# Attention inside a four-part network: denominators from two running totals, counted every sixteen key tiles, two halves of weighted sums between the score sets

## The chip, the cores and the metric

One core of a Trainium2 chip runs the whole network as one program. The metric is the device time of one execution in microseconds. The kernel before took 9539.7 us (median of three runs, 9533.88 to 9544.37).

PE is the matrix engine, PEld its loading of weights, DVE the vector engine, ACT the scalar engine (activations such as the exponential), POOL the general engine, SP the engine that issues transfers. Matmuls write to PSUM[...]; the other engines work between PSUM and the on-chip memory.

## The reference

The input is four images of 64 x 64 pixels with 128 channels. Four stages follow one another, each adding to its input: attention, a recurrent layer, a selective scan, and a mixture of experts. Only attention concerns us here. It normalises the channels, then for four heads of 32 channels:

```
q, k, v = split(x @ w_qkv)                  # 4096 tokens per image
q, k    = l2norm over the tokens (axis 1)
sim     = einsum('bihd,bjhd->bhij', q, k) * 10
attn    = softmax(sim, axis=-1)
out     = einsum('bhij,bjhd->bhid', attn, v)
x       = x + out @ w_out + b_out
```

So for each image and head there are 4096 x 4096 exponentials, a weighted sum of `v` by them, and for each query the sum of its exponentials, the denominator.

## The kernel before, in words

All is fp32 and lies with channels, or keys, on the partitions. A first part normalises and makes q, k and v of all images. The second part, `attend`, takes each image's queries in eight chunks of 512 (`c`), and for each chunk its keys in 32 tiles of 128 (`t`). That is 4 x 8 x 32 = 1024 tiles, each with four units, one for each head. This part's instructions are placed on each engine in the order in which the code emits them (the schedule is written by hand), so the loop's order is the order of the work. The maximum is not subtracted; a bound on the scores that is worked out first lets the small-score version run.

The loop runs in turns. In a turn, `scores("sa", 4)` (L288) makes the next four units' scores, each a matmul of 32 rows, into a tile of four PSUM banks, and one ACT instruction (L303) writes their exponentials into a ring in the on-chip memory. The ring has places for 8 tiles (`RING`) of four heads, 32 places in all, and a set that crosses its end takes two ACT instructions. Then come `halves(BETWEEN)`, the weighted sums (L313): for each tile, two halves of 256 queries, four matmuls each, one for each head. The second part of the turn is `scores("sb", 3)`, a set of three units into three banks, followed by the halves that are left of the turn's four (`HEADS - n`). [...]`sa`, `sb` and `av` have one buffer each: a new set waits until ACT has read the last one. `state["halves"]` rations the halves to the scores made: a full turn makes seven units, which pay for three and a half halves, so turns with four halves alternate with shorter ones.

The denominators go another way. `added` (called for each tile whose scores are done) lets DVE add the tile's 128 x 2048 exponentials into a total: the first two tiles of each eight make it (L332), each further one is added in place (L336). After every `SUMMED` = 8 tiles the total is due to be counted, `LATER` = 3 turns on: in that turn the tile `sb` is not used for scores but for `counted` (L341), four matmuls of the total with ones, which sum over the keys on the partitions. ACT copies the sum to `den` (L351 for a chunk's first count, L353 for the next ones), and DVE adds the later ones up (L354). When a chunk's last total is counted, DVE takes the reciprocal (L358) and multiplies the weighted sum by it (L359), and the next counting turn also holds the projection by `w_out` (L365), with its bias on ACT (L368), the addition of `x` on DVE (L372) and the store (L373).

The ring ties the engines: a place is written again eight tiles later, and before that DVE must have added the tile and PE must have used it.

Of the kernel before, what the change touches and what calls it, by code (L numbers as in the profile page):

```python
# [19 lines left out]
F32 = mybir.dt.float32  # L20
# [6 lines left out]
P = 128  # L27
B, HW, C = 4, 64, 128
L = HW * HW
CH = 512  # L30
# [3 lines left out]
HEADS, DH = 4, 32  # L34
# [131 lines left out]
@with_exitstack  # L166
def attention(ctx, tc, a, x1):

    nc = tc.nc
    flag = ctx.enter_context(tc.tile_pool(name="at_f", bufs=1)).tile(
        [1, 1], mybir.dt.int32, name="flag"
    )
    with ExitStack() as inner:
        attention_of_small(inner, tc, a, x1, flag)
    with tc.If(nc.values_load(flag) > 0):  # L180
        attention_of_any(tc, a, x1)


def attention_of_small(ctx, tc, a, x1, flag):

    nc = tc.nc
    cst = ctx.enter_context(tc.tile_pool(name="at_c", bufs=1))
    NJ = L // P
    RING = 8
    LATER = 3  # L190
    SUMMED = 8
    BETWEEN = 3

    ident = cst.tile([P, P], F32, name="ident")
    make_identity(nc, ident)
# [68 lines left out]
    def attend(stream, work, ps):  # L264
# [11 lines left out]
        def scores(tag, size):  # L276

            s = ps.tile([P, size, CH], F32, tag=tag, name=tag)
            n0, m, done = state["n"], 0, []
            for _ in range(size):  # L280
                unit = next(units, None)
                if unit is None:
                    state["over"] = True
                    break
                chunk_state, t, i = unit
                q, k = chunk_state["qk"]
                rows = slice(DH * i, DH * i + DH)
                nc.tensor.matmul(  # L288
                    s[:, m, :],
                    k[rows, tokens(t)],  # L290
                    q[rows, chunk(chunk_state["c"])],
                    start=True,
                    stop=True,
                )
                m += 1
                if i == HEADS - 1:
                    done.append((chunk_state, t, place(n0 + m - HEADS)))
            state["n"] += m
            at = 0
            while at < m:  # L300
                lo = place(n0 + at)
                n = min(m - at, RING * HEADS - lo)
                nc.scalar.activation(ring[:, lo : lo + n, :], s[:, at : at + n, :], AF.Exp)  # L303
                at += n
            return done
# [18 lines left out]
        def added(chunk_state, t, at):  # L324

            w = ring[:, at : at + HEADS, :]
            g = t % SUMMED
            if g == 0:
                chunk_state["first"] = w
            elif g == 1:  # L330
                total = work.tile([P, HEADS, CH], F32, tag="total", name="total")
                nc.vector.tensor_add(total, chunk_state["first"], w)  # L332
                chunk_state["total"] = total
            else:
                total = chunk_state["total"]
                nc.vector.tensor_add(total, total, w)  # L336
            return g == SUMMED - 1

        def counted(slot, chunk_state, t, total):
            for i in range(HEADS):  # L340
                nc.tensor.matmul(  # L341
                    slot[DH * i : DH * i + DH, 0, :], ones, total[:, i, :], start=True, stop=True
                )
            return lambda: taken(slot, chunk_state, t)

        def taken(slot, chunk_state, t):
            if t < SUMMED:
                chunk_state["den"] = work.tile([P, 2, CH], F32, tag="den", name="den")
            den = chunk_state["den"]
            if t < SUMMED:  # L350
                nc.scalar.copy(den[:, 0, :], slot[:, 0, :])  # L351
            else:
                nc.scalar.copy(den[:, 1, :], slot[:, 0, :])  # L353
                later.append(lambda: nc.vector.tensor_add(den[:, 0, :], den[:, 0, :], den[:, 1, :]))  # L354
# [22 lines left out]
        def halves(limit):  # L377

            n = 0
            while n < limit and state["halves"] > 0 and ready:  # L380
                half = state["half"]
                if n and half == 0 and ready[0][1] == 0:
                    break
                tile = ready[0]
                weighted(half, *tile)
                whole = tile[1] == 0
                if half or whole:
                    ready.pop(0)
                state["half"] = 0 if whole else 1 - half
                state["halves"] -= 4 if whole else 2  # L390
                n += 2 if whole else 1
            return n
# [5 lines left out]
        while ready or to_count or to_divide or to_project or later or not state["over"]:  # L398
            turn += 1
            before = state["n"]  # L400
            done = [] if state["over"] else scores("sa", 4)
            n = halves(BETWEEN)
            ending = state["over"] and not ready and not to_count
            counting = to_count and to_count[0][0] <= turn
            if counting or (to_project and ending):
                slot = ps.tile([P, 3, CH], F32, tag="sb", name="sb")
                after = []
                if counting:
                    _, chunk_state, t, total = to_count.pop(0)
# [13 lines left out]
            for tile_done in done:  # L423
                if added(*tile_done):
                    chunk_state, t, _ = tile_done
                    to_count.append((turn + LATER, chunk_state, t, chunk_state["total"]))
            ready += done
# [1421 lines left out]
```

## Time and profile before

| what | number |
|---|---|
| median of three runs | 9539.7 us |
| the profiled execution's own time | 9539.87 us |
| its span | 9538.1 us |
| PE, DVE, ACT, POOL busy, share of the span | 92%, 88%, 72%, 54% |
| granted PE clock, mean | 0.969 |
| attention's score sets, first and last start | 233.4 and 2627.8 us |
| L336 adds, mean | 768, 2290 ns |
| L332 adds, mean | 128, 2288 ns |
| L303 exponentials of `sa`, mean | 640, 1879 ns |
| L303 exponentials of `sb`, mean | 512, 1452 ns |

Attention with its preparation is the first 2640 us or so of the span; the rest is the other three stages, which the change does not touch. The busy shares of the whole page are means over all stages, so what follows looks at attention alone. A line number is the place in the code from which an instruction comes. A group's row gives the busy time, the mean of one, and the idle time of the engine just ahead of it with what ended it. A matmul in fp32 shows as two records. "issue" is time in which an engine waited for nothing that the profile shows.

### The profile page before, as it was taken

What the parts mean: (1) busy time and instruction counts of PE and PEld (TensorE: products, weight loads), DVE (VectorE), ACT (ScalarE), POOL (GpSimd) and SP (SyncE); (2) the same over time, 40 slices, a digit from 0 to 9 for tenths busy, and PEclk for the clock granted to TensorE, in tenths of its full rate; (3) what the DMA queues carried; (4) which work ended last, traced back from release to release, by engine and by line L of the source; (5) the groups of instructions that cost most, each with busy time, mean ns of one, the idle gap of its engine ahead of it and who ended that gap; (6) DMA issues with size and microseconds to landing.
All of it is one profiled execution on the core that took longest, in us unless ns stands there. A gap on an engine that the chain in (4) does not pass through costs nothing. (4 is left out here: it accounts for less than half of the span.)

```text
span 9538.1 us, 238512 instructions
## 1 busy us (share of the span) xinstructions
PE 8769.6 (92%) x102706; PEld 4347.9 (46%) x102706; DVE 8353.8 (88%) x5099; ACT 6913.6 (72%) x10362; POOL 5157.2 (54%) x2433
## 2 busy tenths in 40 slices
PE   7999999999988888999999999999999999999766
PEld 3333333333323334555555555555555555555223
DVE  6999999999978218999999999999999999999764
ACT  3888888888856457777778877877777777777321
POOL 0000000000001017999999999999999999999100
PEclk8999999999999888999999999999999999999887
DMA  4001000000011335666666666666666666665634
GB/s 173 29 8 37 8 8 34 8 10 8 8 60 51 114 135 150 169 170 170 170 168 161 161 159 159 160 168 171 170 171 170 170 171 171 170 170 164 228 118 182
DMA packets 530961, 1164.79 MB, mean 122 GB/s; under 512 B 76818, under 2 KB 444506, under 8 KB 502106
## 3 DMA queue, kind: packets, MB, share of 16 engines
q1 hardware_dynamic: 529882, 1149.30, 41.6%
q8 instruction: 811, 13.29, 0.6%
q14 instruction: 268, 2.20, 0.1%
HBM read 828.51 MB, written 182.15 MB: 106 GB/s over the span
## 5 line engine op out<-in xcount | busy, mean ns | idle before, releaser
L1288 DVE TENSOR_TENSOR_SCAN states<-decays,db 128x1016 f32<-128x1016 f32 x2112 | 4668.6, 2256 | 100.3 <-ACT decays L1309 60.9
L1322 POOL TENSOR_TENSOR products<-states,c_ring 128x1000 f32<-128x1000 f32 x2112 | 4456.9, 2151 | 219.2 <-PE y L1339 190.4
L1229 ACT ACTIVATE decays<-dt,a_logs 128x500 f32<-128x500 f32 x4224 | 3017.2, 714 | 90.3 <-DVE states L1288 4.2
L1264 PEld LDWEIGHTS db<-b_diag,dtu_t 32*128 32x128 f32 x16896 | 2050.0, 186 | 1607.6 <-DVE states L1288 1187.7
L1264 PE MATMUL db<-b_diag,dtu_t 32*128 32x128 f32 x16896 | 2428.6, 283 | 316.2 <-DVE states L1288 310.5
L1264 PE MATMUL db<-b_other,dtu_t 32*128 32x128 f32 x16896 | 2457.4, 284 | 0.0
L1273 PE MATMUL y<-zeros 32*128 32x128 f32 x14720 | 2122.3, 283 | 0.0
L1264 PEld LDWEIGHTS db<-b_other,dtu_t 32*128 32x128 f32 x16896 | 2048.8, 186 | 0.1
L1339 PE MATMUL y<-products,ident 64*64 64x500 f32 x16896 | 2019.1, 592 | 1.1 <-POOL products L1322 1.1
L336 DVE TENSOR_TENSOR total<-total,ring 128x2048 f32<-128x2048 f32 x768 | 1759.1, 2290 | 66.8 <-DVE total L336 2.3
L1273 PEld LDWEIGHTS y<-zeros 32*128 32x128 f32 x14720 | 1772.1, 186 | 0.0
masks.py:197 POOL MEMSET ident<- 128x128 f32 x6 | 1.2, 205 | 2940.3 <-SPq L180 2647.1
L303 ACT ACTIVATE ring<-sa 128x2048 f32<-128x2048 f32 x640 | 1202.8, 1879 | 159.5 <-PE sa L288 159.4
L313 PE MATMUL av<-ring,v_at 128*32 128x256 f32 (+1 forms) x16128 | 1094.3, 388 | 0.4 <-ACT ring L303 0.4
L313 PEld LDWEIGHTS av<-ring,v_at 128*32 128x32 f32 x16128 | 432.1, 109 | 941.4 <-issue 745.6
L1339 PEld LDWEIGHTS y<-products,ident 64*64 64x64 f32 x16896 | 541.3, 132 | 696.8 <-issue 568.2
L303 ACT ACTIVATE ring<-sb 128x1536 f32<-128x1536 f32 x512 | 743.6, 1452 | 124.7 <-PE sb L288 109.7
L1309 ACT COPY decays<-states 128x8 f32<-128x8 f32 x2048 | 405.2, 198 | 535.1 <-DVE states L1288 519.0
L288 PE MATMUL sa<-q_at,k_at 32*128 32x512 f32 x5120 | 732.2, 641 | 17.0 <-issue 14.1
L288 PE MATMUL sb<-q_at,k_at 32*128 32x512 f32 x3072 | 582.1, 641 | 0.0
L332 DVE TENSOR_TENSOR total<-ring 128x2048 f32<-128x2048 f32 x128 | 292.9, 2288 | 114.6 <-ACT ring L303 114.6
L288 PEld LDWEIGHTS sa<-q_at,k_at 32*128 32x128 f32 x5120 | 201.0, 183 | 378.5 <-ACT ring L303 205.6
(210 smaller groups left out, 7952.9 us busy)
## 6 DMA issues: line engine op xcount, KB each, us to landing
c_ring<-c_rows SPq DMA_DIRECT2D x2112, 250.0 KB, 4.6
b_other<-b_diag SPq DMA_DIRECT2D x264, 512.0 KB, 6.4
weights<-in_w SPq DMA_DIRECT2D x32, 1024.0 KB, 12.6
u<-u_r SPq DMA_DIRECT2D x60, 500.0 KB, 5.6
y_r<-sum SPq DMA_DIRECT2D x60, 500.0 KB, 4.2
u<-u_c SPq DMA_DIRECT2D x60, 500.0 KB, 5.6
y_c<-sum SPq DMA_DIRECT2D x60, 500.0 KB, 4.1
x<-x SPq DMA_DIRECT2D x96, 256.0 KB, 2.6
```

What stands on the lines that cost most here:

```text
L288: nc.tensor.matmul(s[:, m, :], k[rows, tokens(t)], q[rows, chunk(chunk_state["c"])], start=True, stop=True,)
L303: nc.scalar.activation(ring[:, lo : lo + n, :], s[:, at : at + n, :], AF.Exp)
L313: nc.tensor.matmul(chunk_state["av"][rows, some], chunk_state["v"][:, t, rows], ring[:, at + i, some], start=t == 0, stop=t == NJ - 1 and ...
L332: nc.vector.tensor_add(total, chunk_state["first"], w)
L336: nc.vector.tensor_add(total, total, w)
L1229: nc.scalar.activation(to, dt, AF.Exp, scale=scale)
L1264: nc.tensor.matmul(bank.rearrange("p (n t) -> p n t", n=4)[:, :, to : to + 32], v.dtu[rows, h, s, :], b[rows, s, 4 * self.q : 4 * self.q + ...
L1273: nc.tensor.matmul(y[:, idle // 2, :P], zeros[rows], zeros[rows], start=False, stop=False)
L1288: nc.vector.tensor_tensor_scan(order(self.slot(states)), order(self.slot(decays, shift)), order(self.db[:, SKIP + shift :][:, : 2 * LANE]) ...
L1309: nc.scalar.copy(self.edge(later.slot(decays), later.v.into), last)
L1322: nc.gpsimd.tensor_mul(to, h, c)
L1339: nc.tensor.matmul(to, ident[rows, rows], of, start=begins, stop=ends)
```

## The change

Three constants change. `SUMMED` goes from 8 to 16 tiles, so that a chunk has two counts instead of four. `LATER` goes from 3 to 4 turns. `BETWEEN`, the most halves of weighted sums between the two score sets of a turn, goes from 3 to 2; the other two may follow behind the second set.

Within each sixteen tiles there are two totals, one for even and one for odd tiles. Tiles 0 and 1 are only remembered; tile 2 makes the even total from tiles 0 and 2, tile 3 the odd one from 1 and 3; later tiles are added to the two in turn; behind tile 15 one more add joins the two. The even total has two buffers and the odd one a single buffer, each of 128 x 2048; `den` goes from two buffers to one.

```
-    LATER = 3
-    SUMMED = 8
-    BETWEEN = 3
+    LATER = 4
+    SUMMED = 16
+    BETWEEN = 2
...
             g = t % SUMMED
             if g == 0:
-                chunk_state["first"] = w
-            elif g == 1:
-                total = work.tile([P, HEADS, CH], F32, tag="total", name="total")
-                nc.vector.tensor_add(total, chunk_state["first"], w)
-                chunk_state["total"] = total
-            else:
-                total = chunk_state["total"]
-                nc.vector.tensor_add(total, total, w)
-            return g == SUMMED - 1
+                chunk_state["sums"] = []
+            sums = chunk_state["sums"]
+            if g < 2:
+                sums.append(w)
+                return False
+            if g < 4:
+                total = work.tile(
+                    [P, HEADS, CH], F32, tag=f"total{g}", name=f"total{g}", bufs=4 - g
+                )
+                nc.vector.tensor_add(total, sums[g - 2], w)
+                sums[g - 2] = total
+                return False
+            nc.vector.tensor_add(sums[g % 2], sums[g % 2], w)
+            if g < SUMMED - 1:
+                return False
+            nc.vector.tensor_add(sums[0], sums[0], sums[1])
+            chunk_state["total"] = sums[0]
+            return True
...
             if t < SUMMED:
-                chunk_state["den"] = work.tile([P, 2, CH], F32, tag="den", name="den")
+                chunk_state["den"] = work.tile([P, 2, CH], F32, tag="den", name="den", bufs=1)
```

## The prediction

> **What bounds the kernel now.** The change touches only the attention stage, so I asked first where that stage lies and which engine is full in it. The busy time by stretches (length, then busy time and instruction count of each engine) puts it between about 219 us and 2640 us of the 9538.1 us span:
>
> ```profile
> core 0: us, PE busy (x) PEld busy (x) DVE busy (x) ACT busy (x) POOL busy (x), PEclk, DMA share, GB/s
> ...
> 600.00:1000.00 400.00, 400.00 (x4252) 138.82 (x4247) 373.14 (x183) 338.05 (x226) 0.00 (x0) 1.00 0.07 24
> 1000.00:1400.00 400.00, 399.73 (x4244) 138.67 (x4240) 374.54 (x183) 337.89 (x225) 0.00 (x0) 1.00 0.03 9
> ```
>
> PE never rests, DVE is at 93%, ACT at 84%, PE's clock is granted in full and DMA does nearly nothing. Next, the groups by line within 300 to 2600 us (xcount | busy us, mean ns of one | idle before):
>
> ```profile
> L336 DVE TENSOR_TENSOR total<-total,ring 128x2048 f32<-128x2048 f32 x738 | 1690.3, 2290 | 63.2 <-DVE total L336 2.3 <-ACT den L351 0.5 <-DVE total L332 0.5
> L303 ACT ACTIVATE ring<-sa 128x2048 f32<-128x2048 f32 x615 | 1155.8, 1879 | 153.6 <-PE sa L288 153.6
> ...
> L303 ACT ACTIVATE ring<-sb 128x1536 f32<-128x1536 f32 x492 | 714.6, 1452 | 117.7 <-PE sb L288 103.1
> L288 PE MATMUL sa<-q_at,k_at 32*128 32x512 f32 x4920 | 701.3, 640 | 1.1 <-ACT ring L303 1.1
> ...
> L332 DVE TENSOR_TENSOR total<-ring 128x2048 f32<-128x2048 f32 x123 | 281.4, 2288 | 86.9 <-ACT ring L303 86.9
> ```
>
> PE waited 1.1 us in 2300 for score banks; ACT and DVE wait for PE and for ACT. So PE's order of work sets the stage's length. Since matmul ends are modelled, I take PE prices from the starts in the timeline (start, duration, engine, line, group, count):
>
> ```profile
> 1006.50 1.14 PE L288 MATMUL sa<-q_at,k_at 32*128 32x512 f32 x8 [0.27 <-ACT ring L303]
> ...
> 1007.57 1.50 PE L313 MATMUL av<-ring,v_at 128*32 128x256 f32 x24
> ...
> 1008.21 2.28 DVE L336 TENSOR_TENSOR total<-total,ring 128x2048 f32<-128x2048 f32 x1
> 1009.00 1.13 PE L288 MATMUL sb<-q_at,k_at 32*128 32x512 f32 x6
> ...
> 1010.06 0.64 PE L313 MATMUL av<-ring,v_at 128*32 128x256 f32 x8
> ...
> 1010.41 2.28 DVE L332 TENSOR_TENSOR total<-ring 128x2048 f32<-128x2048 f32 x1
> 1010.63 1.14 PE L288 MATMUL sa<-q_at,k_at 32*128 32x512 f32 x8
> ...
> 1012.80 7.09 DVE L336 TENSOR_TENSOR total<-total,ring 128x2048 f32<-128x2048 f32 x3
> ...
> 1013.02 1.04 PE L341 MATMUL sb<-total,ones 128*32 128x512 f32 x8
> ...
> 1013.99 0.30 PEld L365 LDWEIGHTS sb<-o,wo 128*128 128x128 f32 x2 [0.84 <-issue]
> ```
>
> From start to start: a set of scores 1.07 us, whether of four or of three; three halves of weighted sums 1.43, one half 0.57, so 0.43 a half and 0.14 for each group of halves. A turn of set, three halves, set, one half is 4.13; over the stage such turns have a median of 4.14, turns of set, two halves, set 3.15, turns with a count instead of the second set (three halves before it, one after) 3.79, with count and projection 4.99. A count thus costs 3.79 - (1.07 + 1.43 + 0.57) = 0.72, a projection 1.20.
>
> On DVE the same rows show the point about running totals: from an add to a later instruction that does not read its result (L336 at 1008.21 to L332 at 1010.41) 2.20 us; from L332 to the L336 that reads its result 2.39. Over the stage 127 L332-to-L336 steps have a median of 2.39, and an L336 behind a small instruction, which waits for a total finished long before, starts 0.60 us after a 0.68 us add: a wait that is already met costs nothing.
>
> **What the Trainium skill says.** "VectorE: DVE Perf Modes", The TRN2 errata: an fp32 tensor add takes (N+151)/0.96 ns, 2291 at N=2048; the trace has 2290. Its table's 58+N cycles, 2194 ns, fits the trace's 2.20 of an independent follower. The same page, The DRAIN you can't avoid, says a semaphore between two operations costs nothing extra; the trace says 0.19 us (2.39 against 2.20) where it is the result just written, and the trace decides. "ScalarE: Activation LUTs", What ACT_TABLE_LOAD costs: an activation takes 186 ns + 0.833 ns an element, consecutive ones overlapping by some 93 ns; the trace has 1879 (1892 by the formula), and its two sizes give 1452 - 3 x 427 = 171 ns fixed.
>
> **The change, part by part.** The numbers of instructions are from the order of the instructions in the two programs.
>
> 1. Counts on PE: 128 become 64, and each count's turn loses a three-score set. Turns go from 640 to 613, sets from 640+512 = 1152 to 613+549 = 1162. Score matmuls (4096) and halves (2048) are unchanged; groups of halves go from 1022 to 1023. So -64 x 0.72 = -46.1 us and +10 x 1.07 = +10.7 us. The 64 ACT copies (0.59 us) and 64 DVE adds of `den` (0.60 us) that go with them are off PE's path.
>
> 2. BETWEEN 3 to 2: the turn patterns become 365 of 2+2 halves, 181 of 2+0, 45 count turns with 2+2, 18 with 2+0, in place of 256 of 3+1, 255 of 2+0 and 127 count turns of 3+1. A 2+2 turn is 1.07+1.00+1.07+1.00 = 4.13 (rounding), the same as 3+1; the halves only move. The second set directly ahead of the first costs some 0.02 more (3.17 mean against 3.15), 74 times fewer: -1.5 us.
>
> 3. Where PE meets ACT anew: `sa` and `sb` have one buffer each. In a 2+0 turn the next `sa` comes 3.15 us after the last one; that one's exponentials start some 1.21 us after their set and take 1.88, so it is just met, as today. Three new cases are not met. A 2+0 turn behind a 2+0 turn (9 times): exponentials start 0.27 later, stall some 0.25. A count turn with no halves behind it (18 times): next set due at 2.82 to 2.93 against 3.15, stall some 0.3. And the ring's places no longer repeat with the pattern: 90 of the 1162 sets now straddle the ring's end and take two activations, adding 171 ns less the overlap of some 0.1; about a tenth of the 181 tight turns are hit. Together 2 + 5 + 3 = +10 us. The extra ACT work itself (90 x 0.08 = 7 us) hides in ACT's 16% idle.
>
> 4. Adds on DVE: 7 per eight tiles become 15 per sixteen, 896 to 960. Before: 128 x (6 x 2.39 + 2.20) = 2117 us; small instructions 96 x 0.60 + 32 x (3.38 + 0.61 + 0.60) = 204; each of those 160 breaks a chain and saves 0.19, -30: 2291. After: even and odd totals alternate, so 64 x (14 x 2.20 + 2.39) = 2124, small instructions 32 x 0.60 + 147 = 166: 2290. The extra adds are paid by the removed waits. This is the least certain price, since no run shows two alternating totals: bounds 2.20 and 2.39, taken 2.20.
>
> 5. What DVE's lateness can hold up. Setting the adds against the exponentials tile by tile, DVE ends a tile's add 2.3 to 8.2 us after its exponentials (8.2 behind a division), and the ring place is rewritten at least 8.1 us after that. Holding tiles 0 and 1 until tiles 2 and 3 costs one more tile, 2.3 us: still free. LATER 4: the last add plus the merging add of 2.2 to 2.4 ends at most some 10 us behind the exponentials; the count comes four turns on, about 15 us: no wait. `den` with one buffer: the copy for the next chunk comes over ten tiles behind the division: no wait. At the very end the merging add is exposed, about +1 us.
>
> Sum: -46.1 + 10.7 - 1.5 + 10 + 1 = -26 us; 2 us more where a count runs straight into a score set. Against the profiled 9539.87 us, which equals the median of 9539.7 within 0.2, that is some 9512. Work outside the stage is unchanged.
>
> **Rivals.**
> - A, likeliest, 0.77: as summed, 9500 to 9521, the ends being no new ACT stalls (-38) and twice as many (-17).
> - B, no change, 0.13: PE's saving is given back because score sets and exponentials mesh worse: if all 90 straddling sets stall PE 0.15 (+13) and the tight turns that follow another short turn lose 0.5, the gain is some 12 us: 9528. For it: ACT and PE run within 0.1 us of each other in 2+0 turns. Against it: there are fewer such turns than before.
> - C, slower, 0.08: DVE becomes the bound. If each alternating add still costs 2.39, DVE needs 64 x 15 x 2.39 + 166 = 2460 us, and the stage ends near 242 + 2460 = 2702 instead of 2645: 9597. It decides from 2.31 us per add: the adds now run from 242 to 2635, and 64 x (14p + 2.39) + 166 fills those 2393 us at p = 2.31. Against it are the steps of 2.20 and of 0.60 above.
> - D, larger gain, 0.02: 9495, if counts free ACT and DVE in ways that the turn prices miss.
>
> **How the numbers follow.** A difference under 0.2%, 19 us, can't be told from none. A's bulk lies under 9520.6; a small part of it counts as no change. Faster: 0.75 of A and D; same: 0.16; slower: 0.09. The likeliest is 9512; the range 9499 to 9530 holds A and B's centre, and leaves out C and D.
>
> **What would show it.** The profile after should have 64 counts, 613 and 549 score sets, PE still at 99% in the stage, which ends some 26 us sooner; adds on DVE 2.20 us apart with 2.39 only at the merging add; some 90 split activations; waits of `sa` for the ring's exponentials not above some 15 us in PE's own idle. Adds 2.39 apart and PE idle ahead of the counts (L350) or ACT waiting for DVE would show C. PE starts of `sa` held past 3.15 us in most 2+0 turns would show B.

## The result, and the profile after

The changed kernel took 9515.4 us (median of 11 runs, 9496.45 to 9526.49) against 9535.9 us (11 runs) before: a ratio of 0.9974, 95% interval 0.9965 to 0.9983. It is faster by 0.26%, a little more than can be told from no change. The forecast was 9512 us.

The profiled execution has a span of 9515.2 us, 22.9 us less than before. Where it went is best read from the attention stage itself, from its first weight load for scores (233.36 us before, 233.71 after) to the issue of its last store. In the timeline of the kernel before (start, duration, engine, line, transfer):

```profile
2645.12 0.32 SPq L373 DMA_DIRECT2D x<-x_at  x1
```

and of the changed kernel:

```profile
2621.21 0.32 SPq L382 DMA_DIRECT2D x<-x_at  x1
```

So the stage went from 2645.12 - 233.36 = 2411.8 us to 2387.5 us: 24.3 us shorter. What lies outside it is 7126.3 us before and 7127.7 after. That rest is identical code in all the kernels of this study, and in their ten profiles it takes 7107 to 7130 us. The stage is steadier: the one pair of kernels with the same PE work took 2411.8 and 2411.9 us, and a full turn of the loop has a median of 4.14 us in every profile. So most readings below are made on the stage. It has two parts. Up to ACT's copy of the last accumulator (L322) PE works almost without a pause: 2398.5 us before, 2371.7 after, 26.7 less. The end from there to the last store went from 13.3 to 15.8 us, 2.5 more.

The same stretches of the changed kernel, with the busy time of each engine:

```profile
core 0: us, PE busy (x) PEld busy (x) DVE busy (x) ACT busy (x) POOL busy (x), PEclk, DMA share, GB/s
...
600.00:1000.00 400.00, 398.47 (x4212) 136.38 (x4208) 386.66 (x184) 336.84 (x235) 0.00 (x0) 1.00 0.07 24
1000.00:1400.00 400.00, 397.64 (x4203) 136.09 (x4204) 386.81 (x185) 335.76 (x233) 0.00 (x0) 1.00 0.03 8
```

PE is still full, though with some 2 us of idle time in 400 where there was next to none. DVE shows 387 us busy where it showed 373, yet it has not become the limit, and that looks odd until its instructions are seen in order. In the timeline, around a division:

```profile
1000.65 0.69 DVE L368 TENSOR_TENSOR o<-o,den 128x512 f32<-128x512 f32 x1
1001.26 17.70 DVE L341 TENSOR_TENSOR total<-total,ring 128x2048 f32<-128x2048 f32 x8
...
1019.00 2.29 DVE L344 TENSOR_TENSOR total<-total,total 128x2048 f32<-128x2048 f32 x1
...
1021.21 4.49 DVE L338 TENSOR_TENSOR total<-ring 128x2048 f32<-128x2048 f32 x2
```

Eight adds that alternate between the totals take 17.70 us up to the last one's end: (17.70 - 2.29)/7 = 2.20 us from start to start. Each thus starts some 0.09 us ahead of the end of the one before it. The add that joins the totals reads the last one's result and starts 0.04 us behind its end (1018.96 to 1019.00); the next group, which doesn't read it, starts 2.21 us after its start, ahead of its end again. A record lasts 2.29 us however close the next one starts, so busy time counts more adds in the same stretch without showing that each of them takes 0.19 us less from start to start.

The groups by line for 300 to 2580 us (xcount | busy us, mean ns | idle before):

```profile
L341 DVE TENSOR_TENSOR total<-total,ring 128x2048 f32<-128x2048 f32 x738 | 1640.2, 2285 | 29.6 <-ACT ring L303 28.9
...
L303 ACT ACTIVATE ring<-sa 128x2048 f32<-128x2048 f32 x539 | 1012.6, 1879 | 230.5 <-PE sa L288 218.9 <-DVE total L341 7.7 <-DVE total L338 3.2
...
L288 PE MATMUL sa<-q_at,k_at 32*128 32x512 f32 x4720 | 672.9, 640 | 4.2 <-ACT ring L303 1.5
...
L338 DVE TENSOR_TENSOR total<-ring 128x2048 f32<-128x2048 f32 x124 | 279.5, 2287 | 40.9 <-ACT ring L303 40.6
L344 DVE TENSOR_TENSOR total<-total,total 128x2048 f32<-128x2048 f32 x62 | 142.1, 2292 | 2.1
L350 PE MATMUL sb<-total,ones 128*32 128x512 f32 x488 | 63.5, 592 | 0.0
```

The in-place adds used to have 63.2 us of gaps, nearly all between chained adds (each reads the result of the one before); now nearly all their idle time is a wait for exponentials. DVE still waits for data at the start of a group (40.9 us), which means that it keeps up. The counts (L350) are half as many, with no idle time ahead of them: no count waits for a total there (only the very last one does, behind all the work). The few microseconds that the row of `sa` puts down to a total on DVE aren't waits for ring places. When each of the stage's 1252 exponentials' instructions is set beside the add that had freed its place, none starts less than 5.8 us behind the end of that add (8.1 us in the kernel before).

### The profile page after: what moved, and what is told of

Read it like the earlier page. It is cut to its first block, busy times and chain, and to the rows that moved or that the text cites. A ratio compares the mean times of both kernels' runs of the same rounds, so it can differ in the third digit from the quotient of the medians.

```text
span 9515.2 us, 237518 instructions
## 1 busy us (share of the span) xinstructions
PE 8735.5 (92%) x102194; PEld 4329.6 (46%) x102194; DVE 8414.2 (88%) x5099; ACT 6880.6 (72%) x10398; POOL 5155.1 (54%) x2433
## 5 line engine op out<-in xcount | busy, mean ns | idle before, releaser
L341 DVE TENSOR_TENSOR total<-total,ring 128x2048 f32<-128x2048 f32 x768 | 1706.9, 2285 | 32.5 <-ACT ring L303 31.8
L303 ACT ACTIVATE ring<-sa 128x2048 f32<-128x2048 f32 (+3 forms) x667 | 1153.5, 1738 | 274.2 <-PE sa L288 262.6
L303 ACT ACTIVATE ring<-sb 128x1536 f32<-128x1536 f32 (+2 forms) x585 | 800.5, 1375 | 73.8 <-PE sb L288 63.9
L288 PE MATMUL sa<-q_at,k_at 32*128 32x512 f32 x4898 | 701.4, 641 | 20.3 <-issue 14.1
L288 PE MATMUL sb<-q_at,k_at 32*128 32x512 f32 x3294 | 624.1, 641 | 0.0
```

Of the source, the lines that this page charges most:

```text
L288: nc.tensor.matmul(s[:, m, :], k[rows, tokens(t)], q[rows, chunk(chunk_state["c"])], start=True, stop=True,)
L341: nc.vector.tensor_add(sums[g % 2], sums[g % 2], w)
```

## The experiments

Three explanations were on the table. The first, mine, is that PE's order sets the length: fewer counts, less the price of ten more score sets, bring the gain, and the two totals only keep DVE out of the way. The second is that the waits between DVE's adds held the stage back. The third is that the place of the halves, two between the score sets, covers ACT better. All stage lengths are from one profiled execution, first weight load to last store; each ratio is against runs of the kernel before that were made beside those of the kernel in its row.

| kernel | stage, us | ratio to before, 95% |
|---|---|---|
| before | 2411.8 | |
| changed | 2387.5 | 0.9974, 0.9965 to 0.9983 |
| changed, one total | 2453.7 | 1.0049, 1.0035 to 1.0063 |
| before, two totals | 2407.7 | 0.9999, 0.9990 to 1.0007 |
| before, BETWEEN 2 | 2411.9 | 1.0001, 0.9992 to 1.0009 |
| before, a count every 4 tiles | 2616.3 | 1.0224, 1.0210 to 1.0238 |
| changed, BETWEEN 3 | 2392.5 | 0.9977, 0.9969 to 0.9985 |
| changed, LATER 3 | 2399.9 | 0.9986, 0.9980 to 0.9993 |
| changed, a count every 32 tiles | 2368.0 | 0.9950, 0.9936 to 0.9963 |
| before, first set's exponentials split | 2435.4 | one run |

### One total in place of two

```
-            nc.vector.tensor_add(sums[g % 2], sums[g % 2], w)
-            if g < SUMMED - 1:
-                return False
-            nc.vector.tensor_add(sums[0], sums[0], sums[1])
...
+            else:
+                total = chunk_state["total"]
+                nc.vector.tensor_add(total, total, w)
+            return g == SUMMED - 1
```

> The changed kernel, but with one running total over the sixteen tiles, added in place, as in the kernel before (15 adds, 14 of them behind the add whose result they read). My theory: PE's order is that of the changed kernel, but DVE becomes the bound: 64 x (14 x 2.39 + 2.20) = 2282 us of adds, 148 us of small instructions behind broken chains, 2430 us from 242 us on, so the attention stage ends near 2678 us instead of 2645 and the time is some 9565 us (9550 to 9585); DVE over 99% busy or chained in the stage, PE idle. Rival, that fewer counts are all that matters and the two totals do nothing: 9512 us like the changed kernel.

The median was 9578.9 us (9562.96 to 9581.1). PE has the changed kernel's work, and yet the stage is 66 us longer than with two totals and 42 us longer than before. The timeline of this kernel behind a division shows the reason:

```profile
1015.84 3.34 DVE L358 RECIPROCAL den<-den 128x512 f32<-128x512 f32 x1
1019.22 0.69 DVE L359 TENSOR_TENSOR o<-o,den 128x512 f32<-128x512 f32 x1
1019.83 19.06 DVE L336 TENSOR_TENSOR total<-total,ring 128x2048 f32<-128x2048 f32 x8
1029.40 1.88 ACT L303 ACTIVATE ring<-sa 128x2048 f32<-128x2048 f32 x1 [0.92 <-DVE total L336]
1031.79 1.45 ACT L303 ACTIVATE ring<-sb 128x1536 f32<-128x1536 f32 x1 [0.52 <-DVE total L336]
...
1039.03 1.06 PE L341 MATMUL sb<-total,ones 128*32 128x512 f32 x8 [0.77 <-DVE total L336]
```

Eight chained adds now take 19.06 us, (19.06 - 2.29)/7 = 2.40 each. DVE falls so far behind that ACT waits for ring places (99 of its exponentials' instructions start within 0.2 us of the end of the add that freed their place) and PE waits for the total that it is to count: this is rival C of the prediction, brought about by taking the second total away. DVE shows only 386 us busy in 400 all the same, about as much as in the changed kernel, since the 0.11 us between two chained adds counts as idle. Of the two ways of adding up sixteen tiles that were run, only the alternating one keeps up.

### Two totals alone

The diff is against the changed kernel: its code with the constants of the kernel before.

```
-    LATER = 4
-    SUMMED = 16
-    BETWEEN = 2
+    LATER = 3
+    SUMMED = 8
+    BETWEEN = 3
```

> The kernel before with two totals, even and odd, joined every eight tiles (and the single den buffer that makes room for them); counts, LATER and BETWEEN as before. My theory: DVE has 128 x (6 x 2.20 + 2.39) = 1995 us of adds instead of 2117, and nothing changes because PE sets the length: 9536 us, within 5 us; DVE idles some 120 us more. Rival, that the waits between adds held the kernel back: 9515 us or less.

9533.0 us against 9535.0, ratio 0.9999: no change that can be told. DVE's spare time is longer. From the waits of this kernel for 300 to 2580 us (who waited for whom, total us, times, longest):

```profile
DVE total L338 <- ACT ring L303: 144.2, 91, 1.9
...
DVE total L341 <- ACT ring L303: 24.9, 92, 0.3
```

Of the idle time of 144 and 25 us that these rows give, the kernel before has 86.9 us, all ahead of a group's first add (for 300 to 2600 us). That is 82 us more, not the 120 expected: that sum left out that DVE's small instructions already broke the chain of adds in many places, which the prediction had put at 30 us. The stage itself is 4.1 us shorter. Up to the copy of the last accumulator it gains 6.4 us: some 90 waits of 0.06 us of the four-unit set for ACT are gone. At the end it loses 2.3, since the joining add comes on top there. What made ACT 0.06 us earlier was not found; ring places it was not, as they were free at least 7.4 us ahead in this kernel and 8.1 in the kernel before. The second total is thus worth some 4 us by itself.

### The place of the halves

```
-    BETWEEN = 3
+    BETWEEN = 2
```

> The kernel before with BETWEEN = 2 alone: 256 turns of 2+2 halves in the place of 3+1. My theory: the same PE work in another place, 9536 us within 5 us. Rival, that the halves' place brings the gain because ACT's reading of the first set is better covered: 9515 us.

9537.1 us, ratio 1.0001, and a stage of 2411.9 us against 2411.8: 256 turns with their halves moved, and nothing lost or gained. In the changed kernel the constant was put back:

```
-    BETWEEN = 2
+    BETWEEN = 3
```

> The changed kernel with BETWEEN back at 3: 353 turns of 3+1 halves instead of 365 of 2+2, the same 64 counts, 613 + 549 sets and 1252 exponential instructions. My theory: the halves' place is worth nothing, so the attention stage, 2387.5 us from its first score set to its last store in the changed kernel's profile, stays within 4 us of that, and the time is some 24 us under the kernel before, within 6 us. Rival, that two halves between the sets brought part of the gain: 2395 us or more.

The median was 9515.4 us. The stage is 2392.5 us, 5.0 more, just outside the 4 us that I had stated; the medians of the runs don't show a difference. A row of the waits for 300 to 2580 us tells which wait grew; the changed kernel first, then this one:

```profile
PE av L313 <- ACT o L322: 5.7, 12, 0.6
```

```profile
PE av L313 <- ACT o L322: 12.0, 27, 0.6
```

At a chunk's start the accumulator `av` must first be copied by ACT. In the kernel before, PE's idle ahead of these halves was nil, since eight tiles are exactly five turns and the chunk's end always falls on the same place in a turn. With a count every sixteen tiles it drifts, and with three halves ahead of the second set it meets the copy more often. Two halves are worth some 5 us here, by this wait and not by covering the first set.

### More counts

```
-    SUMMED = 8
+    SUMMED = 4
```

> The kernel before with a count every four tiles (SUMMED = 4): 256 counts instead of 128, 1136 score sets instead of 1152, 768 DVE adds of exponentials instead of 896. My theory: PE pays 128 x 0.72 = 92 us for counts and saves 16 x 1.07 = 17 us of sets; with some 10 to 20 us for count turns that have no halves behind the count, 9536 + 75 to 95 = 9611 to 9631 us. Rival, that DVE is a bound beside PE: it saves some 230 us of DVE work, so less than half of that rise, or a gain.

The sign decides between the first two explanations: DVE loses 128 adds and is busy 310 us in 400, and the kernel is 2.2% slower. The size was far off: the stage grew by 204.6 us and not by 75 to 95. The price of counts and sets is 92 - 17 = 75 us; the rest I had put at 10 to 20. Adding up, over all PE starts, what each step took beyond its price gives 135 us where the kernel before has 18, so 75 + 117 = 192 of the 204.6 us are accounted for. Most of the 117 us is idle time of PE. Two rows of the waits for 300 to 2580 us:

```profile
PE sb L365 <- DVE o L359: 50.6, 20, 5.3
PE sa L288 <- ACT ring L303: 29.4, 88, 0.5
```

The second row lies mostly in the 63 count turns in which a score set follows the count directly. The first is a projection that waits for its division, as here:

```profile
1058.53 3.35 DVE L358 RECIPROCAL den<-den 128x512 f32<-128x512 f32 x1
1061.90 0.69 DVE L359 TENSOR_TENSOR o<-o,den 128x512 f32<-128x512 f32 x1
...
1062.65 2.08 PE L365 MATMUL sb<-o,wo 128*128 128x512 f32 x2 [3.32 <-DVE o L359]
...
1064.66 2.09 PE L288 MATMUL sa<-q_at,k_at 32*128 32x512 f32 x8
```

The projection rides in the next counting turn. With a count every four tiles that turn comes before DVE has divided, and PE stands still. With eight tiles or more between counts the division is done by then, and in the kernels before and changed PE's rows ahead of the projection show no wait for it.

The wait also has an aftermath. The projection takes 2.08 us here, against 1.12 us in the changed kernel, where PE came to it without a pause, and the score set behind it 2.09 us against 1.14. The granted PE clock (PEclk, the third number from the end) is low in this stretch; it is 1.00 in the 4 us ahead of it and again from 1070 us on:

```profile
1062.00:1066.00 4.00, 3.35 (x10) 1.02 (x10) 2.82 (x3) 1.18 (x2) 0.00 (x0) 0.52 0.00 0
```

Thirteen such stretches of 3.5 to 7.5 us lie between 300 and 2840 us, where the kernel before has none up to its last turn. PE's steps in them took some 26 us more than their prices, the waits themselves apart. A long stall of PE is thus paid twice, and prices that are read from a PE that never rests miss the second part.

### An earlier count

```
-    LATER = 4
+    LATER = 3
```

> The changed kernel with LATER = 3, one turn (3.8 us) less between the joined total and its count. My theory: the joined total ends at most 10.4 us behind the last exponentials and the count comes 11 us or more behind them, so at most some counts wait a fraction of a us: the stage stays within 5 us of the changed kernel's 2387.5 us. Rival, that the later count is needed because the joining add makes the total late: each of 64 counts waits 1 us or more, 2450 us or more.

The median was 9522.9 us. The stage is 2399.9 us, 12.4 more than with LATER = 4: more than my bound of 5, far from the rival's 62 and more. A row of its waits for 300 to 2580 us shows PE's idle time ahead of the counts (L350):

```profile
PE sb L350 <- DVE total L344: 10.0, 8, 1.9
```

Only some of the 64 counts wait, those behind a division, where the joined total ends late, up to 10.7 us behind the last exponentials. I had taken every count to come 11 us or more behind them; with three turns some were due after 8.6 us. So the fourth turn is part of the gain: without it half of the gain is lost. `LATER` = 4 alone, in the kernel before, was not run; PE has no idle time ahead of the counts there (L341, 0.0 us of 128.1 busy for 300 to 2600 us), so there was nothing for it to save.

### Straddling sets

In the kernel before, each four-unit set's exponentials are split into one unit and three:

```
                 n = min(m - at, RING * HEADS - lo)
+                if tag == "sa" and at == 0:
+                    n = 1
```

> The kernel before, with the exponentials of each four-unit set taken in two ACT instructions (one unit, then three), as happens in the changed kernel where a set straddles the ring's end: 640 more activations. My theory: the set's exponentials end 0.07 to 0.17 us later, which only the 255 turns of 2+0 halves feel, where the next set waits for them: the attention stage grows from 2411.8 us by 18 to 43 us, and PE's stalls sit ahead of the four-unit set in those turns. Rival, that ACT is close enough to its limit that a split costs 0.1 us or more wherever it is: 64 us or more.

The stage grew by 23.6 us, inside the range expected. Of the 255 turns of 2+0 halves 251 now take 3.26 us, where in the kernel before half took 3.14 us (the next set comes just in time) and nearly all others 3.20 (it waits a little for ACT); all other turns stayed at 4.14, 3.79 and 4.99. So a split costs 0.12 or 0.06 us where the next set is close on ACT's heels, and nothing elsewhere. For 640 extra activations that is 0.04 us each, and an estimate of some 3 us for the 90 of the changed kernel. Only sets of four were split here; what a split set of three costs was not tested.

### One count for a chunk

```
-    SUMMED = 16
+    SUMMED = 32
```

> The changed kernel with SUMMED = 32: one count for a chunk, 32 in all, 600 + 566 score sets instead of 613 + 549. My theory: PE saves 32 x 0.72 = 23 us more and pays 4 x 1.07 = 4 us, so the stage is some 2368 us (2362 to 2374) and the time some 44 us under the kernel before. DVE then has 32 x (30 x 2.20 + 2.39) + 147 = 2335 us of work, 98.9% of the stage. Rival, that DVE at that load holds ring places or counts up: no shorter than the changed kernel's 2387.5 us, with PE waiting for DVE ahead of counts or ACT waiting for DVE.

9488.9 us (9487.49 to 9494.13), ratio 0.9950; the stage is 2368.0 us, 43.8 less than before and 19.5 less than the changed kernel, where the prices give 19. The busy times:

```profile
600.00:1000.00 400.00, 398.60 (x4196) 135.70 (x4188) 397.96 (x187) 337.49 (x232) 0.00 (x0) 1.00 0.07 25
1000.00:1400.00 400.00, 398.20 (x4216) 136.19 (x4216) 398.75 (x187) 337.27 (x233) 0.00 (x0) 1.00 0.03 8
```

and its waits for 300 to 2580 us:

```profile
DVE total L341 <- ACT ring L303: 7.1, 14, 1.8
...
DVE total L338 <- ACT ring L303: 0.5, 1, 0.5
```

DVE now waits for exponentials only 8 us in 2280, and still no ring place is awaited: each was free 5.8 us or more ahead. What DVE's load does cost shows at the end, where nothing covers the last total. The last count of the changed kernel, then of this one:

```profile
2610.13 1.94 PE L350 MATMUL sb<-total,ones 128*32 128x512 f32 x8 [4.76 <-DVE total L344]
```

```profile
2585.53 1.93 PE L350 MATMUL sb<-total,ones 128*32 128x512 f32 x8 [9.20 <-DVE total L344]
```

Up to the copy of the last accumulator this kernel is 26.5 us shorter than the changed one; at the end, where one more projection is also left, it gives 7.0 us back. The prices had neither part, so their agreement to half a microsecond is partly luck. This version beats both kernels, and with one count for a chunk and DVE this full there is little left for a further step of this kind.

## Why the prediction was right

**Counts and sets (step 1).** Expected -46.1 + 10.7 us. The order has 64 counts and 613 + 549 sets as stated; count turns of four halves took 3.79 us and with projection 4.99, as before. The step is borne out beyond its own case by the count every 32 tiles: -19 us by the same prices, -26.5 measured up to the copy of the last accumulator and -19.5 with the end.

**Halves (step 2).** Turns of 2+2 took a median of 4.14 us, turns of 2+0 3.15, as taken. In the kernel before the move is worth 0.1 us. That it saves 5 us together with rare counts I had not seen. The 0.02 us by which the mean of 2+0 turns lies above 3.15 is no price of two sets in a row, as I took it: in the kernel before 123 of them took 0.06 us and four 0.34 us longer than the rest, waiting for ACT.

**New meetings with ACT (step 3).** Expected +10 us. Adding up the steps that took longer than their price, without the stage's first and last ones, gives 17.7 us in the changed kernel and 9.7 before: +8. What the prediction named came as told: nine 2+0 turns behind another one stalled 0.25 us each; ten count turns without a second group of halves took 3.14 us (2.82 to 2.93 and a stall of 0.3; the eight with a projection took 3.99 and didn't stall); and 36 tight turns, twice the tenth foreseen, have a split set and took 0.06 to 0.12 us longer, 4 us in all. Two terms were not named. The waits of 0.06 and 0.34 us told of in step 2, 9 us before, shrank to 1 us (18 turns without a split). And some 6 us came anew, 12 times 0.5 to 0.7 us between a second score set and the first halves of a new chunk, for ACT's copy of `av`. That these two nearly cancel was luck.

**Adds (step 4).** Expected 2.20 us for alternating adds; 2.20 measured, and 2.40 when one total is chained. The least certain price stood at the end that I took, and the experiment with one total shows what the other end costs.

**Lateness (step 5).** No ring place is awaited in the changed kernel, and no count but the last, as stated. The margin was thinner than told: I gave the joined total 10 us and the count 15; the total ended up to 10.6 us behind the exponentials and the counts came from 12.7 us on, so that one turn less is enough for waits worth 12 us.

**Sum.** Expected -24 to -26 us on the profiled execution, +1 of it at the end; the stage moved by -24.3, +2.5 of it at the end. The median of the runs moved by 20.5, in which the rest of the program, 7107 to 7130 us from one execution to the next, has its share; the kernel before, which the forecast put at 9539.9 us, has a median of 9535.9 over 11 runs. Of the rivals, B stayed away: 63 of the 2+0 turns were held past 3.15 us, where the kernel before has 127. C appears as soon as the second total is taken away.

The Trainium skill's "VectorE: DVE Perf Modes", in The DRAIN you can't avoid, reports that a semaphore behind each of eight tensor copies cost nothing extra. For adds that read the result just written the runs here show otherwise: 2.40 us chained, 2.20 alternating.

## What to carry to other kernels

Price the sequence of the engine that never rests from start to start, and ask of each edit which of its entries disappear; work saved on a busy neighbour is worth nothing until that neighbour is the one waited for. When an accumulation on DVE is too slow, let two accumulators alternate: the same number of adds gets shorter by the wait for the result, and busy time won't show it. Work that goes at a fixed distance behind its source needs that distance set from the worst lateness, here behind a division, not from the mean.

## What was not expected of the hardware

The stage of the kernel before with `BETWEEN` = 2 took 2411.9 us against 2411.8, in another session and with the halves elsewhere, while the rest of the program, the same in all kernels, took 7107 to 7130 us. A few microseconds in one stage can thus be read from two profiles where the times of whole runs can't tell them; for more than this pair it was not tried.

And a PE that had stood still for 3.32 us came back with a granted clock of 0.52, at which a score set took 2.09 us instead of 1.14.
